# Moving small steps of two attention layers from VectorE to ScalarE, with both halves of a sum in one PSUM tile

## The chip, the cores and the metric

The kernel runs on one core of one Trainium2 chip. The core has five engines, each with its own queue that is worked off in order: PE (TensorE, the matmuls; PEld is its loading of weights), DVE (VectorE), ACT (ScalarE), POOL (GpSimd, here mostly the issue of gathers) and SP (SyncE, the queue of plain transfers). The metric is the device time of one execution in microseconds. One execution was also recorded by the hardware profiler; all durations below are from that record. Lines such as L1364 are lines of the kernel before.

## The reference

The reference is a stack of four graph layers on 3327 nodes with 512 features and one dense 0/1 adjacency matrix with rather few ones. Every layer ends in a residual and a layer norm:

```python
x = _layernorm(x + _L0_gnn_ref(x, adj, W, a1, a2))      # attention, 8 heads of 64
x = _layernorm(x + _L1_gnn_ref(x, adj, ...))            # mean of the neighbours
x = _layernorm(x + _L2_gnn_ref(x, adj, ..., 64))        # mean of the first 64
x = _layernorm(x + _L3_gnn_ref(x, adj, W, a))           # attention, 4 heads of 128

# an attention layer
e = leaky_relu(f1[:, :, None] + f2[:, None, :], 0.2)    # by head, node, neighbour
attention = softmax(where(adj > 0, e, NEG_INF))
out = elu(einsum('hnm,hmo->hno', attention, Wh))

def _layernorm(x):
    return (x - mean(x)) / sqrt(var(x) + 1e-5)
```

Layers 0 and 3 are attention layers, and the change touches these two only.

## The kernel before, in words

The nodes are cut into 26 blocks of 128. For each block the kernel first makes a list of the columns in which the block's rows have a one. A block's list is cut into chunks of 128 places, and up to four chunks make a group (`GROUP`). For each layer there is a table in DRAM with one row per node. An attention layer's row holds, for every head, the projected features and two scores.

**One group** (`Gat.group`, a generator that gives way after each stage) runs as follows. POOL issues one indirect gather per chunk (L1018) into a slot of a ring in SBUF. ACT and DVE make, from list positions, a 0/1 matrix that tells which row of the block each place belongs to (`far` L1316 on ACT, `ds` L1324 and L1326 on DVE). PE multiplies it with the block's own scores (`pg`, L1336 in layer 0 and L1340 in layer 3). DVE adds the neighbours' scores and takes the larger of two (L1353, L1355). ACT takes the exponential twice: once as `w` in PSUM (L1356) and once into the score's column of the gathered rows (L1357), from which the softmax's denominator comes. ACT also makes `sel`, the 0/1 matrix as floats (L1359 or L1361). DVE then multiplies every gathered unit, that is one head's features of one chunk, with its weight (L1364; a group of g chunks has g times 8 units in layer 0, g times 4 in layer 3). At last PE multiplies `sel` with the weighted rows (L1383) and adds into two halves of the heads, `acc[0]` and `acc[1]`. In layer 3 each block's last chunk is preceded by products with the first block as a column (L1380), whose factors come from DVE (`upc`, L1420).

**The halves of a sum.** `Gat.sums` takes two PSUM tiles of one bank each under a tag `acc0` or `acc1`; blocks take turns between the tags. In the last blocks of layer 0 the first block is done densely (`open_dense`, `dense`): its sums (`acct`) hold the tag `acc1`, and all other blocks use the other one.

**The end of a block** (`Gat.summed`, `divided`): DVE takes the two denominators, one instruction for each half (`rden`, L1528), and the reciprocal of both (L1529). ACT divides, head by head (L1532, eight in layer 0, four in layer 3), and makes the exponential of the ELU (L1542). DVE puts together ELU and residual in two passes (L1544, L1546); the second one also gives the row's sum. DVE makes minus the mean from it (`nm`, L1547). ACT squares the difference and sums it (L1548). The inverse root is made by POOL in layer 0 (L1553, L1554) and by ACT and DVE in layer 3 (L1558 to L1564). `scaled_by_act` makes the shift, minus the mean times the inverse root, on DVE (L854), and ACT applies scale and shift (L855). In layer 3 that is the output and SP stores it; in layer 0 the new rows are transposed by PE and multiplied with layer 1's weights (L789, L806).

**What sets the order.** Up to the end of layer 0 a scheduler orders every engine's instructions by its own estimates; there the list building for later blocks runs between the attention of earlier ones. From layer 1 on the order is the one in which the program issues them (`manual_schedule`): the generators of `work` (groups) and `ends` (ends of blocks) are stepped in turn, so the order on each queue is fixed by their `yield`s. Layer 3 starts when layer 2 is done and is the last.

Of the kernel before, what the change touches and what calls it, by code (L numbers as in the profile page):

```python
# [8 lines left out]
F32 = mybir.dt.float32  # L9
# [8 lines left out]
AF = mybir.ActivationFunctionType  # L18
ALU = mybir.AluOpType
# [4 lines left out]
P = 128  # L24
# [581 lines left out]
class Sums(list):  # L606

    turn = 0
# [23 lines left out]
def sparse_path(ctx, tc, flag_i, x, adj, l0_w, l0_a1, l0_a2, l1_w_self, l1_b_self, l1_w_nb, l1_b_nb,  # L632
# [13 lines left out]
    nc = tc.nc  # L646
    N, D = x.shape
# [11 lines left out]
    def pool_in(lay, name, bufs=1, **kw):  # L659
        return lay.enter_context(tc.tile_pool(name=name, bufs=bufs, reuse_waits="tile", **kw))  # L660
# [7 lines left out]
    for b in range(NB):  # L668
        lists.append([])
        if b:  # L670
            n = SEGMENTS[b]
# [179 lines left out]
        nc.vector.tensor_scalar(o, y, mv[:, 0:1], rs, ALU.subtract, ALU.mult)  # L851

    def scaled_by_act(o, y, nm, rs):
        nc.vector.tensor_mul(nm[:, 0:1], nm[:, 0:1], rs)  # L854
        nc.scalar.activation(o, y, AF.Identity, bias=nm[:, 0:1], scale=rs)  # L855


# [181 lines left out]
    class Gat:  # L1039
# [250 lines left out]
        def group(self, item, pools, accs, done, sall=None):  # L1290

            b, l, c0, g, at = item
            ring, sp, pacc, pone = pools
            H, OUT, M = self.H, self.OUT, self.M
            hh = H // 2
# [4 lines left out]
            m = l.places(c0 + g - 1, whole)  # L1300
# [12 lines left out]
            for t, k, q0, q1 in parts:  # L1313
                if q0 < q1:
                    o = t[:, q0 * P:q1 * P] if t is far else t[:, :(q1 - q0) * P]
# [5 lines left out]
            for t, k, q0, q1 in parts:  # L1321
                o, dk = ds[:, q0 * P:q1 * P], dgs[:, l.at, k:k + 1]
# [7 lines left out]
            n = 1 if self.k else 3  # L1330
            pe = pg[:, :GROUP * n * 2 * H].rearrange("p (c k h) -> p c h k", c=GROUP, k=n)
            w = pg[:, GROUP * n * 2 * H:GROUP * (2 * n + 1) * H].rearrange("p (c h) -> p c h", c=GROUP)
# [27 lines left out]
            else:  # L1360
                nc.scalar.activation(S[:, :g], have, AF.Identity)  # L1361
            yield
            Gc = G.rearrange("p c (h m) -> p (c h) m", m=M)
            nc.vector.tensor_mul(Gc[:, :, :OUT], Gc[:, :, :OUT],  # L1364
                                 w[:, :g].rearrange("p c (h o) -> p (c h) o", o=1).to_broadcast([P, g * H, OUT]))
            yield
            while self.held[self.turn] if at == 0 else b not in accs:
                yield
# [3 lines left out]
            for c in range(g):  # L1372
                m = l.places(c0 + c, whole)
# [50 lines left out]
        def sums(self, pacc, turn):  # L1424

            hh = self.H // 2
            self.held[turn] = 1
            acc = Sums(pacc.tile([P, 512], F32, name="acc", tag=f"acc{turn}")[:, :hh * self.M]
                       .rearrange("p (h m) -> p h m", h=hh) for s in range(2))
            acc.turn = turn  # L1430
            return acc

        def open_dense(self, pool, ps, pacc, *spaces):

            H, OUT, M = self.H, self.OUT, self.M
            hh = H // 2
            self.pinned, self.turn = True, 0
            self.up, *self.wt = [t.rearrange("p (h i) -> p h i", i=P) for t in spaces[:3]]  # L1440
            self.gd = spaces[3:]
            f1 = pool.tile([P, H], F32, name="f1c")
            nc.vector.tensor_add(f1, self.fall[:, :H, 0], self.cmax)
            for h in range(H):
                nc.vector.tensor_scalar(self.wt[0][:, h, :], ident, f1[:, h:h + 1], None, ALU.mult)
            yield
            for s in range(2):
                pf = ps.tile([P, hh * P], F32, name="pf", tag="po")
                nc.tensor.matmul(pf, ones, self.wt[0][:, s * hh:(s + 1) * hh], start=True, stop=True)
                nc.scalar.activation(self.up[:, s * hh:(s + 1) * hh], pf.rearrange("p (h i) -> p h i", i=P),  # L1450
                                     AF.Exp, scale=1.0 - GAT_ALPHA)
                yield
            while self.held[1]:
                yield
            self.nil = pool.tile([1, OUT + 1], F32, name="nil")
            nc.vector.memset(self.nil, 0.0)
            self.acc = [pacc.tile([P, hh * P], F32, name="acct", tag="acc1") for s in range(2)]
            for s in range(2):
                nc.tensor.matmul(self.acc[s][:OUT + 1], self.nil, self.up[0:1, s * hh:(s + 1) * hh],
                                 start=True, stop=False)  # L1460
            self.opened = True
# [59 lines left out]
        def divided(self, fin, acc, h):  # L1521

            H, OUT = self.H, self.OUT
            hh = H // 2
            h = h.rearrange("p (s h o) -> p s h o", s=2, h=hh)
            rden = fin.tile([P, 2, hh, 1], F32, name="rden")
            for s in range(2):
                nc.vector.tensor_scalar(rden[:, s], acc[s][:, :, OUT:OUT + 1], 1e-30, None, ALU.max)  # L1528
            nc.vector.reciprocal(rden, rden)  # L1529
            for s in range(2):  # L1530
                for k in range(hh):
                    nc.scalar.activation(h[:, s, k], acc[s][:, k, :OUT], AF.Identity, scale=rden[:, s, k])  # L1532

        def summed(self, fin, acc, xb, space=None):

            hq = acc
            if isinstance(acc, list):
                hq = fin.tile([P, D], F32, name="h") if space is None else space[:, :D]
                self.divided(fin, acc, hq)
                self.held[acc.turn] = 0  # L1540
            e = fin.tile([P, D], F32, name="e") if space is None else space[:, D:]
            nc.scalar.activation(e, hq, AF.Exp)  # L1542
            yield
            nc.vector.scalar_tensor_tensor(hq, hq, 0.0, xb, ALU.max, ALU.add)  # L1544
            nm = fin.tile([P, 2], F32, name="nm")
            nc.vector.scalar_tensor_tensor(e, e, 1.0, hq, ALU.min, ALU.add, accum_out=nm[:, 0:1])  # L1546
            nc.vector.tensor_scalar(nm[:, 0:1], nm[:, 0:1], -1.0 / D, None, ALU.mult)  # L1547
            nc.scalar.activation(hq, e, AF.Square, bias=nm[:, 0:1], accum_out=nm[:, 1:2])  # L1548
            if self.k == 0:
                for _ in range(AHEAD):  # L1550
                    yield
                rs = fin.tile([P, 1], F32, name="rs")
                nc.gpsimd.tensor_scalar(rs, nm[:, 1:2], 1.0 / D, EPS, ALU.mult, ALU.add)  # L1553
                nc.gpsimd.tensor_tensor(rs, rs, mhalf, ALU.pow)  # L1554
                yield
            else:
                r0 = fin.tile([P, 1], F32, name="r0")
                nc.scalar.activation(r0, nm[:, 1:2], AF.Ln, bias=eps, scale=1.0 / D)  # L1558
                nc.scalar.activation(r0, r0, AF.Exp, scale=-0.5)
                yield  # L1560
                rs = fin.tile([P, 1], F32, name="rs")
                nc.vector.scalar_tensor_tensor(rs, nm[:, 1:2], EPS * D, r0, ALU.add, ALU.mult)
                nc.vector.scalar_tensor_tensor(rs, rs, -0.5 / D, r0, ALU.mult, ALU.mult)
                nc.vector.scalar_tensor_tensor(rs, rs, 1.5, r0, ALU.add, ALU.mult)  # L1564
            return e, nm, rs
# [167 lines left out]
    def layer0_end(b, acc):  # L1733
        yield
        x1 = xres[b]
        space = None
        if b == order[-1]:
            while g0.pinned:
                yield
            space = dp.tile([P, H0 * P], F32, name="up")  # L1740
        e, nm, rs = yield from g0.summed(fin, acc, x1, space)
        scaled_by_act(x1, e, nm, rs)
        xt = None
        if space is not None:
            xt = dp.tile([P, H0 * g0.M], F32, name="gd2")[:, :D].rearrange("p (c i) -> p c i", i=P)
        xt = transposed(fin, ps, x1, xt=xt)
        yield
        t2 = fin.tile([P, 2, D], F32R, name="t2", bufs=2)
        po = times(ps, xt, wn)
        nc.scalar.copy(t2[:, 0], po)  # L1750
        nc.vector.tensor_sub(t2[:, 1], po, t2[:, 0].bitcast(F32))
        store(t1_d, b, t2.bitcast(F32).rearrange("p s d -> p (s d)"), 2)
        if b >= NB - LATE0 or not b:
            return
        yield
        zb = fin.tile([P, D], F32, name="zb0", tag="e")
        nc.scalar.copy(zb, times(ps, xt, wx))
        store(z1_d, b, zb)
# [150 lines left out]
    pacc = pool_in(mlay, "l1pa", 2, space=PSUM)  # L1909
# [237 lines left out]
    with ExitStack() as lay:  # L2147
# [7 lines left out]
        def layer3_end(b, acc):  # L2155
            yield
            e, nm, rs = yield from g3.summed(fin, acc, xres[b])
            o = fin.tile([P, D], F32, name="o")
            scaled_by_act(o, e, nm, rs)
            store(out, b, o)  # L2160
# [82 lines left out]
```

## Time and profile before

| what | us |
|---|---|
| median of 4 runs (lowest, highest) | 1757.98 (1748.88, 1762.15) |
| the profiled execution's own time | 1759.4 |
| its span in the profile | 1757.6 |
| busy in the span: PE | 1514.4 (86%) |
| DVE | 1181.8 (67%) |
| ACT | 866.8 (49%) |
| POOL | 752.2 (43%) |
| L1364 in layer 0, 33 groups of 1536 elements (270 to 740 us) | 57.7, mean 1.748 |
| L1364 in layer 3, 24 groups of 1536 elements in one ring part (1480 to 1757 us) | 41.9, mean 1.745 |
| L1547 in layer 0, 26 times | 3.8, mean 0.146 |
| L854 in layer 0, 26 times | 4.0, mean 0.153 |
| L1528 in layer 0, 52 times | 7.6, mean 0.155 |

The span is the time from the first to the last instruction; the profiled execution's own time has 1.8 us more around it. An engine's busy time is a sum over the whole span, in which the four layers have different limits: layer 0's attention lies between about 270 and 740 us, layers 1 and 2 between 740 and 1480, layer 3 behind. So the share of a stretch says more than the share of the span. The profile's chain of waits names the work that ended last at each moment; over the span it is 64% PE, 11% DVE and 7% ACT.

### The profile page before, as it was taken

To read this page: it belongs to the slowest core of one execution; us is meant where nothing else is said; L and a number is where in the kernel's file an instruction comes from. 1 tells how busy PE (TensorE), PEld (TensorE's weight loads), DVE (VectorE), ACT (ScalarE), POOL (GpSimd) and SP (SyncE) were. 2 spreads that over 40 slices of the span, in tenths; PEclk is the share of its full clock that TensorE was granted. 3 is DMA by queue.
4 is the path that set the end of the run, shared out by engine and by line. 5 is a ranking of instruction groups with operands and counts; after the bars stand their busy time and mean duration, and the time that the engine had idled before them with its cause. 6 is when DMAs were issued, how large, how long until landed. Compare 5 with 4: busy or idle time off the path is not lost.

```text
span 1757.6 us, 24418 instructions
## 1 busy us (share of the span) xinstructions
PE 1514.4 (86%) x7307; PEld 1012.4 (58%) x7341; DVE 1181.8 (67%) x3210; ACT 866.8 (49%) x2907; POOL 752.2 (43%) x992
## 2 busy tenths in 40 slices
PE   5789937889999999889999999967999984878885
PEld 4667625656666677545555555423676652756664
DVE  7997857878566789225656776565455553867897
ACT  5788744666666778412212212212444442545686
POOL 2000055555554421163545553276555506666650
PEclk9889968889999999889999999998999995988998
DMA  8877667666664542297888997388767706667771
GB/s 258 266 237 242 211 212 235 212 193 191 207 183 148 170 145 74 94 399 272 291 286 303 339 367 244 99 294 259 244 209 241 256 25 200 183 203 211 215 214 61
DMA packets 120794, 382.01 MB, mean 217 GB/s; under 512 B 22028, under 2 KB 23668, under 8 KB 120650
## 3 DMA queue, kind: packets, MB, share of 16 engines
q0 software_dynamic: 67696, 252.97, 45.7%
q1 hardware_dynamic: 52954, 127.35, 21.6%
q8 instruction: 61, 1.00, 0.2%
q14 instruction: 83, 0.68, 0.1%
HBM read 331.89 MB, written 48.37 MB: 216 GB/s over the span
## 4 chain that ended last, share of the span: by engine, by line
PE 64%; DVE 11%; ACT 7%; issue 7%; DMA 5%; another core or an unknown queue 3%; POOL 3%; SPq 0%; POOLq 0%; ACTq 0%; DVEq 0%
PE po L806 19%; PE acc L1383 13%; PE po L1056 10%; PE acc L1893 9%; PE pt L789 3%; PE acct L1491 1%; PE acc L1885 1%; PE acc L1271 1%; ACT m L882 1%; DVE gt L1364 1%; DVE gl L1364 1%; DMA gt<-t_d,idx 1%; PE acc L1976 1%; DMA ab<-in_adj_dram 1%
## 5 line engine op out<-in xcount | busy, mean ns | idle before, releaser
L1018 POOL DMA_INDIRECT gt<-t_d,idx x201 | 199.4, 992 | 381.3 <-DVE eq L978 209.0
L1018 POOL DMA_INDIRECT gl<-t_d,idx x265 | 263.3, 993 | 201.0 <-issue 57.4
L1383 PE MATMUL acc<-gt,sel 128*128 128x264 f32 (+3 forms) x804 | 213.6, 413 | 4.2 <-issue 2.1
L1018 POOL DMA_INDIRECT gm<-t_d,idx x140 | 140.6, 1004 | 139.7 <-PE acc L1893 89.8
L806 PE MATMUL po<-wn,xt 128*128 128x512 f32 x408 | 194.0, 618 | 7.3 <-ACT xt L792 5.0
L1383 PEld LDWEIGHTS acc<-gt,sel 128*128 128x128 f32 (+3 forms) x804 | 155.3, 202 | 46.0 <-issue 18.2
L1383 PE MATMUL acc<-gl,sel 128*128 128x260 f32 (+3 forms) x524 | 139.1, 409 | 27.6 <-issue 16.8
L1056 PE MATMUL po<-gt,xt 128*128 128x268 f32 x416 | 119.4, 433 | 12.7 <-ACT g0fall L1068 8.2
L806 PEld LDWEIGHTS po<-wn,xt 128*128 128x128 f32 x408 | 77.6, 198 | 91.5 <-issue 82.0
L1364 DVE TENSOR_TENSOR gt<-gt,pg 128x1536 f32<-128x1536 f32 (+3 forms) x64 | 116.6, 1822 | 17.3 <-ACT sel L1359 14.6
L1383 PEld LDWEIGHTS acc<-gl,sel 128*128 128x128 f32 (+3 forms) x524 | 99.4, 200 | 46.6 <-issue 20.1
L796 ACT ACTIVATE xt<-pt 128x128 f32<-128x128 f32 (+1 forms) x208 | 55.8, 291 | 116.9 <-PE pt L789 77.4
L1056 PE MATMUL po<-w,xt 128*128 128x262 f32 x416 | 100.5, 393 | 13.8 <-issue 7.6
L1893 PE MATMUL acc<-gm,selr 128*128 128x512 f32 (+3 forms) x324 | 107.2, 454 | 5.2 <-DMA gm<-t_d,idx 3.8
L792 ACT COPY xt<-pt 128x512 f32<-128x512 f32 x80 | 46.8, 589 | 126.7 <-PE pt L789 103.0
L909 DVE MAX8 cand<-val 128x8 f32<-128x464 uint16 (+32 forms) x184 | 107.5, 619 | 0.1
L1018 POOL DMA_INDIRECT gk<-t_d,idx x65 | 65.6, 1009 | 89.1 <-PE acc L1271 51.6
L789 PE MATMUL pt<-s_ident,xres 128*128 128x128 f32 x500 | 79.1, 286 | 27.0 <-DMA xres<-in_x_dram 12.2
L1316 ACT ACTIVATE far<-place,sites 128x128 int16<-128x128 int16 (+3 forms) x167 | 87.0, 542 | 27.7 <-DVE ds L1326 24.4
L1056 PEld LDWEIGHTS po<-gt,xt 128*128 128x128 f32 x416 | 80.3, 206 | 31.7 <-ACT g0fall L1068 8.6
L806 PE MATMUL po<-wx,xt 128*128 128x512 f32 x208 | 94.3, 597 | 1.7 <-ACT tb L1938 1.2
L1056 PEld LDWEIGHTS po<-w,xt 128*128 128x128 f32 x416 | 78.2, 193 | 29.9 <-issue 9.9
(406 smaller groups left out, 3260.8 us busy)
## 6 DMA issues: line engine op xcount, KB each, us to landing
ab<-in_adj_dram SPq DMA_DIRECT2D x25, 832.0 KB
ab<-in_adj_dram SPq DMA_DIRECT2D x25, 831.5 KB
t_d<-t SPq DMA_DIRECT2D x25, 512.0 KB
gm<-t_d POOLq DMA_DIRECT2D x21, 512.0 KB
t_d<-t SPq DMA_DIRECT2D x25, 384.0 KB
t_d<-tg SPq DMA_DIRECT2D x25, 264.0 KB
gd<-t_d SPq DMA_DIRECT2D x25, 264.0 KB
t_d<-tg SPq DMA_DIRECT2D x25, 260.0 KB
```

Source lines behind the costliest of these rows:

```text
L789: nc.tensor.transpose(pt[:, c, :], src[:, c * P:(c + 1) * P], ident)
L792: nc.scalar.copy(xt, pt)
L796: nc.scalar.activation(xt[:, c, :n], pt[:, c, :n], AF.Identity, accum_out=xsum[:, c, b:b + 1])
L806: nc.tensor.matmul(po, xt[:, c, :], w[:, c], start=c == 0, stop=c == DC - 1)
L882: nc.scalar.activation(m[:, c0:], ab[s][:, c0:], AF.Sign, accum_out=half[:, s, b:b + 1])
L909: nc.vector.max(out=cand[:, s, :], in_=val[:, cuts[s]:cuts[s + 1]])
L1018: nc.gpsimd.indirect_dma_start(out=t[:m, c, :], out_offset=None, in_=table[:, :], in_offset=bass.IndirectOffsetOnAxis(ap=l.idx[:m, c0 + c: ...
L1056: nc.tensor.matmul(pw[s], xt[:, c, :], self.w[:, c, s, :], start=c == 0, stop=c == DC - 1)
L1316: nc.scalar.activation(o, place[:, (c0 + q0) * P:(c0 + q1) * P], AF.Abs, bias=l.nmid[k], scale=2.0)
L1364: nc.vector.tensor_mul(Gc[:, :, :OUT], Gc[:, :, :OUT], w[:, :g].rearrange("p c (h o) -> p (c h) o", o=1).to_broadcast([P, g * H, OUT]))
L1383: nc.tensor.matmul(accs[b][s], S[:m, c, :], G[:m, c, s * hh * M:(s + 1) * hh * M], start=at + c == 0, stop=last)
L1893: nc.tensor.matmul(accs[b], chosen, parts[:, k * D:(k + 1) * D], start=at + c + k == 0, stop=k == top and at + c == n - 1)
```

## The change

The change has four parts.

1. Minus the mean (L1547) and the shift (L854) are made by ACT, with an activation that scales, and no longer by DVE. Both layers use these lines.
2. The two halves of a block's sums are one PSUM tile of two banks, with one buffer for each tag; the dense sums of layer 0 likewise. A tile is guarded as a whole: it comes free when all that read it are done.
3. With both halves in one tile DVE takes both denominators in one instruction.
4. In layer 3 (`self.k` is 1 there and 0 in layer 0) DVE weights all units of a group but the last; ACT weights that one, with the weight that it has put into the score's column itself.

```diff
     def scaled_by_act(o, y, nm, rs):
-        nc.vector.tensor_mul(nm[:, 0:1], nm[:, 0:1], rs)
+        nc.scalar.activation(nm[:, 0:1], nm[:, 0:1], AF.Identity, scale=rs)
         nc.scalar.activation(o, y, AF.Identity, bias=nm[:, 0:1], scale=rs)
...
             Gc = G.rearrange("p c (h m) -> p (c h) m", m=M)
-            nc.vector.tensor_mul(Gc[:, :, :OUT], Gc[:, :, :OUT],
-                                 w[:, :g].rearrange("p c (h o) -> p (c h) o", o=1).to_broadcast([P, g * H, OUT]))
+            n = g * H - self.k
+            nc.vector.tensor_mul(Gc[:, :n, :OUT], Gc[:, :n, :OUT],
+                                 w[:, :g].rearrange("p c (h o) -> p (c h) o", o=1)[:, :n].to_broadcast([P, n, OUT]))
+            if n < g * H:
+                nc.scalar.activation(Gc[:, n, :OUT], Gc[:, n, :OUT], AF.Identity, scale=Gc[:, n, OUT:OUT + 1])
...
-            acc = Sums(pacc.tile([P, 512], F32, name="acc", tag=f"acc{turn}")[:, :hh * self.M]
-                       .rearrange("p (h m) -> p h m", h=hh) for s in range(2))
+            both = pacc.tile([P, 2, 512], F32, name="acc", tag=f"acc{turn}", bufs=1)
+            acc = Sums(both[:, s, :hh * self.M].rearrange("p (h m) -> p h m", h=hh) for s in range(2))
             acc.turn = turn
+            acc.both = both[:, :, :hh * self.M].rearrange("p s (h m) -> p s h m", h=hh)
...
-            self.acc = [pacc.tile([P, hh * P], F32, name="acct", tag="acc1") for s in range(2)]
+            acct = pacc.tile([P, 2, 512], F32, name="acct", tag="acc1", bufs=1)
+            self.acc = [acct[:, s, :hh * P] for s in range(2)]
...
-            for s in range(2):
-                nc.vector.tensor_scalar(rden[:, s], acc[s][:, :, OUT:OUT + 1], 1e-30, None, ALU.max)
+            if isinstance(acc, Sums):
+                nc.vector.tensor_scalar(rden, acc.both[:, :, :, OUT:OUT + 1], 1e-30, None, ALU.max)
+            else:
+                for s in range(2):
+                    nc.vector.tensor_scalar(rden[:, s], acc[s][:, :, OUT:OUT + 1], 1e-30, None, ALU.max)
...
-            nc.vector.tensor_scalar(nm[:, 0:1], nm[:, 0:1], -1.0 / D, None, ALU.mult)
+            nc.scalar.activation(nm[:, 0:1], nm[:, 0:1], AF.Identity, scale=-1.0 / D)
```

## The prediction

> **What bounds the kernel now.** I read the busy time by stretches first, to find where DVE, the engine that the change relieves, could be the one that ends last. Columns: length, then busy us of PE, PEld, DVE, ACT, POOL, then granted clock, DMA share, GB/s.
>
> ```profile
> 270.00:400.00 130.00, 107.14 (x565) 76.33 (x563) 105.80 (x317) 77.92 (x229) 71.73 (x76) 0.88 0.68 209
> 400.00:640.00 240.00, 230.38 (x1113) 159.36 (x1112) 166.15 (x419) 165.38 (x545) 116.78 (x135) 0.98 0.59 178
> 640.00:740.00 100.00, 93.96 (x495) 66.30 (x495) 69.80 (x145) 70.95 (x264) 10.30 (x15) 0.95 0.24 77
> ```
>
> ```profile
> 1545.00:1660.00 115.00, 96.63 (x600) 78.42 (x600) 89.12 (x258) 69.86 (x212) 72.80 (x75) 0.90 0.73 207
> 1660.00:1740.00 80.00, 64.12 (x440) 53.22 (x439) 74.06 (x233) 61.93 (x194) 29.96 (x31) 1.00 0.56 165
> ```
>
> The first three are layer 0's attention, the last two layer 3's. From 400 to 640 PE is busy 230.4 of 240 us: nothing taken from DVE there shortens the span by more than PE's idle 9.6 us. PE's idle time is 22.9 us in 270-400 and 6.0 us in 640-740. Only in 1660-1740 is DVE the busiest (74.1 of 80), with ACT close behind (61.9). So I read that stretch instruction by instruction. Columns: start, duration, engine, line, operation, tiles, shapes.
>
> ```profile
> 1676.80 0.17 DVE L1355 TENSOR_TENSOR sc<-sc 128x12 f32<-128x12 f32 x1
> ...
> 1677.11 0.22 DVE L1528 TENSOR_SCALAR rden<-acc 128x2 f32<-128x2 f32 x2
> ...
> 1677.81 0.16 DVE L1564 SCALAR_TENSOR_TENSOR rs<-rs,r 128x1 f32<-128x1 f32 x1
> 1678.01 0.16 DVE L854 TENSOR_TENSOR nm<-nm,rs 128x1 f32<-128x1 f32 x1
> 1678.08 1.75 DVE L1364 TENSOR_TENSOR gl<-gl,pg 128x1536 f32<-128x1536 f32 x1
> ...
> 1680.25 0.69 DVE L1544 SCALAR_TENSOR_TENSOR h<-h,xres 128x512 f32<-128x512 f32 x1
> ...
> 1681.59 0.08 DVE L1546 DVE_READ_ACCUMULATOR e<-e,h 128x1 f32 x1
> 1681.71 0.15 DVE L1547 TENSOR_SCALAR nm<-nm 128x1 f32<-128x1 f32 x1
> 1681.78 1.13 DVE L1420 SCALAR_TENSOR_TENSOR upc<-upc,least,col 128x128 f32<-128x128 f32 x4
> ```
>
> ```profile
> 1677.06 0.18 ACT L1356 ACTIVATE pg<-sc 128x12 f32<-128x12 f32 x1 [1.17 <-remote]
> ...
> 1679.59 0.63 ACT L1542 ACTIVATE e<-h 128x512 f32<-128x512 f32 x1
> 1680.12 0.80 ACT L855 ACTIVATE o<-e,nm,rs 128x512 f32<-128x512 f32 x1
> ...
> 1683.07 0.20 ACT L1559 ACTIVATE r<-r 128x1 f32<-128x1 f32 x1
> 1684.44 0.18 ACT L1356 ACTIVATE pg<-sc 128x12 f32<-128x12 f32 x1 [1.17 <-DVE sc L1353]
> ```
>
> The reader is to see a loop, once per block: ACT's exponential (L1356, 1677.06) runs on to e (L1542, ends 1680.22), which DVE's L1544 follows at 1680.25: **leg A, 3.19 us**. DVE then runs L1544, L1546, L1547, L1420, L1364 and the scores, and ACT's next exponential starts at 1684.44: **leg B, 4.19 us**. Together 7.38 us a block (7.58 in the next, which has one more 0.2 us zero copy on ACT). In leg B ACT idles 1.17 us before that exponential.
>
> **The change, part by part.** Line numbers are those of the kernel before. PE, POOL and SP keep their instructions. In the built program DVE loses 155: 52 of L854, 52 of L1547 (26 blocks in each of two layers) and 51 of L1528. ACT gains 104 in place of the first two, and 57 weightings.
>
> *Layer 3, DVE.* L1364 loses 128 of its elements. The groups of 1536 and 2048 elements took 1.747 and 2.277 us, so 512 elements cost 0.530 and 128 cost 0.13 us. L1547 leaves: L1420 started 0.07 us after it, and it 0.12 after the accumulator read; without it I put 0.10 saved. L854 leaves: it started 0.20 after L1564 on which it depended, and L1364 does not, so about 0.13 to 0.20 goes. Two L1528 of 2 columns become one of 4 (about 0.1 less). Per block with two groups: 0.26 + 0.10 + 0.2 + 0.1 = 0.66 us of DVE.
>
> *Layer 3, ACT.* It gains two 128x1 operations and two 128x128 weightings a block. For the first the nearest rows are L1559 (0.20 us) and the 128x8 ones of L1479 (0.207); followed by what depends on them I put 0.22 each. For the second it is the same operation on another tile:
>
> ```profile
> L1408 ACT ACTIVATE gcol<-gcol x4: 386/386/388, 1467.9 to 1468.7; 128x128 f32<-128x128 f32 x4
> ```
>
> Four of them in a row started 0.27 us apart, so 0.27 is what a queue of independent work pays and 0.39 the other end. I take 0.27, since the weighting stands between independent operations. Sum 2 x 0.22 + 2 x 0.27 = 0.98 us; by the upper ends 2 x 0.21 + 2 x 0.39 = 1.2.
>
> *Both together in the loop.* All four new ACT operations fall into leg B: the built order has L854 before L855, a weighting before each L1356, and L1547 before the square. Leg A keeps its ACT work, 3.19. Leg B on DVE is 4.19 - 0.10 - 0.13 = 3.96 (only one of the two L1364 is in it). Leg B on ACT, start to start in the trace: L855 0.71, two exponentials 0.19, sel 0.31, far 0.57, square and its read 0.84, Ln 0.33, Exp 0.11: 3.06; with the new work 4.04, begun 0.13 before leg B, so over at 3.91. The two engines end almost together and the loop takes 7.15 to 7.2 in place of 7.38. **I take 0.2 us a block**, on the nine full periods of the tail: -1.8 us. Most of DVE's 0.66 is not on the path: what goes in leg A is covered by ACT's 3.19.
>
> The Trainium skill ("ScalarE: Activation LUTs", Rules for kernel authors) speaks against the move: multiplications belong on VectorE, and an ACTIVATE should be budgeted at some 0.3 us and 0.83 ns an element. Estimated by that page the four would cost 2 x 0.3 + 2 x 0.41 = 1.42 us, leg B on ACT would be 4.35 and the loop 7.54, a loss of 0.16 a block. The rows above are shorter, so the sum stays with them.
>
> *From 1545 to 1660* the loop is a different one: PE waits for L1364, and DVE's scores wait for PE (PE restarts at 1640.39 and 1649.52, with 4.9 of the 9.1 us on DVE). 0.10 + 0.13 = 0.23 us a block is on it. Ten blocks end here; PE is at full load in some and at half clock in others, so I count half: -1.2 (ends 0 and -2.3). Between 1497 and 1545 gathers and PE decide: 0. At the very end each last block's chain keeps two more hops inside ACT: 2 x 0.05, +0.1.
>
> *PE's new wait.* The last matmul of a group now waits for ACT's weighting too; behind it stands PE's whole queue. The weighting before the first L1356 comes 1.2 us after PE starts that group's 2.9 us, and only the product of the last chunk's second half needs it. Cost nothing; with that cover gone, up to 0.3 us a block.
>
> *Layer 0.* DVE loses 26 x (0.15 + 0.15 + 0.15) = 11.7 us, ACT gains 26 x 0.4 = 10. DVE also loses a stall:
>
> ```profile
> DVE nm L854 <- POOL rs L1554: 17.0, 15, 2.0
> ```
>
> (us in all, times, longest.) ACT inherits this wait; L855, right behind L854, had it already through DVE (10.7 us in 10 waits). In 400-640 PE covers all of it. Four blocks end in 270-400, where PE waited 10.3 us for L1364: 4 x 0.3 = -1.2. Six end in 640-740 with ACT as full as DVE (70.9 and 69.8): I put -0.8. The single guard of both halves makes a block's first matmul wait for eight L1532 instead of four, some 4 x 0.24 = 1 us, but two turns alternate and PE has dense products between; nothing, or +1 for each of six blocks. Layer 0's order is made by the scheduler, and it moves: at two places, the list building around 300-400 and the dense part's end, matmuls swap by a few tens. I cannot price that from rows beyond the idle time: -6 to +4, taken as 0. Layer 0: **-2**.
>
> **Sum:** -1.8 - 1.2 + 0.1 - 2.0 = -4.9 us, from the profiled execution's 1759.4 us (span 1757.6) to **1754.5**; from the median of the four runs, 1758.0, it would be 1753.
>
> **Rivals.** *DVE alone decides.* If ACT's new work hides wholly and leg A follows DVE, the tail gains 0.66 on nine blocks (-5.9), 1545-1660 -2.3, layer 0 -2 to -8 by PE's waits for DVE: about -13, 1746. For it: DVE 93% busy in the tail. Against: e ended 0.03 us before L1544 started, so ACT holds leg A. *ACT takes over (slower).* If each new operation costs its full duration and 0.1 us of hand-over, 1.2 + 0.4 = 1.6 us in place of 0.98, leg B on ACT ends at 4.53; it decides from 4.19, that is from 1.26 us of added work. That is 0.34 on 21 blocks, +7, and in layer 0's dense end 6 x 0.4 = +2.4: 1769. For it: 61.9 us of ACT already in 80. Against: the 0.27 us spacing. *Nothing moves:* PE, gathers and clock set the end and what is gained is waited for: 1759.
>
> **How the numbers follow.** Forecast 0.48, DVE alone 0.22, ACT takes over 0.16, nothing 0.14. A measurement of this kernel can tell about 0.5% (8.8 us) from no change. The forecast's own spread (-9 to 0) gives 0.04 to faster; so faster 0.26, within 0.5% 0.58, slower 0.16. The range 1744 to 1767 takes in the first rival and most of the second.
>
> **What would show it.** Right: in the tail L1544 follows L1544 by 7.15 to 7.45 us, ACT's wait before L1356 falls from 1.17 to under 0.2, and L1364 of 12 units takes 1.61. Wrong: ACT's wait stays near 1 us (gain larger), or DVE waits for ACT at the scores (loss); layer 0's end (last L1554 at 721.6 us) moved by over 4 us shows that the scheduler's order mattered.

## The result and the profile after

The changed kernel takes **1759.39 us** (median of 52 runs, 1751.62 to 1768.79) against 1755.76 us of the kernel before (78 runs, 1744.17 to 1770.58): ratio **1.0019, 95% interval 1.0008 to 1.0031**. It is slower by some 3 us. The forecast was 5 us of gain: the range held, the sign did not. Two later measurements of both kernels gave 1.0023 (1.0006 to 1.0041) and 1.0007 (0.9979 to 1.0034).

The profiled execution after has a span of 1760.5 us (1757.6 before). In the kernel after, lines from L1364 on lie a little lower: the weighting by DVE is L1365 and that by ACT L1368, the products L1386, the denominators of both halves L1533 (at least 1e-30 each), the division L1540, e L1550, the two ELU passes L1552 and L1554, minus the mean L1555, POOL's root L1561 and L1562, the dense products L1496, their closing L1513 and the dense transposes L1521.

Busy time by stretches of the kernel after (columns as in the prediction: length, PE, PEld, DVE, ACT, POOL, clock, DMA share, GB/s):

```profile
270.00:400.00 130.00, 103.83 (x579) 75.02 (x579) 107.19 (x316) 80.92 (x241) 73.35 (x77) 0.95 0.69 209
400.00:640.00 240.00, 229.50 (x1112) 158.28 (x1110) 163.22 (x367) 173.58 (x586) 124.03 (x136) 0.99 0.59 177
640.00:740.00 100.00, 88.69 (x457) 63.45 (x456) 62.30 (x117) 68.18 (x256) 7.53 (x13) 0.90 0.21 67
1545.00:1660.00 115.00, 94.14 (x585) 75.61 (x584) 81.55 (x217) 78.54 (x247) 73.35 (x76) 0.89 0.73 211
1660.00:1740.00 80.00, 68.45 (x451) 55.13 (x450) 68.88 (x206) 72.12 (x239) 32.92 (x34) 0.96 0.62 176
```

In layer 3's tail (last line) the load moved as the change says: DVE 74.1 to 68.9, ACT 61.9 to 72.1, and PE is busy 4.3 us longer in the same 80 us, with 451 matmuls for 440; a part of the 4.3 us is the lower clock (0.96 for 1.00). In layer 0's end (640 to 740) it is the other way round: PE does 457 matmuls for 495 and is busy 5.3 us less, although its clock is lower (0.90 for 0.95), and no other engine is fuller than before.

Periods of the tail's loop after, first DVE, then ACT (start, duration, engine, line, operation, tiles; in brackets idle time and releaser):

```profile
1680.73 0.16 DVE L1572 SCALAR_TENSOR_TENSOR rs<-rs,r 128x1 f32<-128x1 f32 x1
1680.81 1.61 DVE L1365 TENSOR_TENSOR gl<-gl,pg 128x1408 f32<-128x1408 f32 x1
...
1683.22 0.69 DVE L1552 SCALAR_TENSOR_TENSOR h<-h,xres 128x512 f32<-128x512 f32 x1 [0.32 <-issue]
...
1690.59 0.69 DVE L1552 SCALAR_TENSOR_TENSOR h<-h,xres 128x512 f32<-128x512 f32 x1 [0.54 <-issue]
...
1705.58 0.69 DVE L1552 SCALAR_TENSOR_TENSOR h<-h,xres 128x512 f32<-128x512 f32 x1 [0.42 <-issue]
...
1714.65 0.69 DVE L1552 SCALAR_TENSOR_TENSOR h<-h,xres 128x512 f32<-128x512 f32 x1 [0.53 <-ACT e L1550]
```

```profile
1680.04 0.18 ACT L1356 ACTIVATE pg<-sc 128x12 f32<-128x12 f32 x1 [0.51 <-DVE sc L1355]
...
1683.10 0.28 ACT L854 ACTIVATE nm<-nm,rs 128x1 f32<-128x1 f32 x1
1683.41 0.81 ACT L855 ACTIVATE o<-e,nm,rs 128x512 f32<-128x512 f32 x1
1684.13 0.39 ACT L1368 ACTIVATE gl<-gl 128x128 f32<-128x128 f32 x1
1684.42 0.16 ACT L1356 ACTIVATE pg<-sc 128x8 f32<-128x8 f32 x1
...
1687.23 0.16 ACT L1356 ACTIVATE pg<-sc 128x12 f32<-128x12 f32 x1
...
1711.05 0.18 ACT L1356 ACTIVATE pg<-sc 128x12 f32<-128x12 f32 x1 [1.37 <-PE pg L1340]
```

L1552 follows L1552 by 7.37 us (before 7.58 at the same place, with two zero copies on ACT), ACT's wait ahead of L1356 has gone from 1.17 to 0.51 and then to nothing, and now it is DVE that idles ahead of L1552. The last two DVE lines and the last ACT line show a period that went otherwise: it takes 9.07 us, and in it ACT waits 1.37 us for PE. With it the tail as a whole, from the first ELU pass of the eleventh block from the end to the end of the span, takes 77.3 us for 77.4 before.

In layer 0 the last two roots on POOL started at 721.62 and 725.62 us before and at 726.61 and 731.05 after (the 721.6 in the prediction, called the last, is the last but one). At layer 0's last gather the kernel after was still ahead: it started at 639.6 us, that of before at 645.1. So these two traces, one of each kernel, put what was lost into layer 0's end; layer 3 won a part of it back: from its first product with weighted rows (at 1473.0 us, before at 1466.5) to the end of the span it took 287.5 us for 291.2.

### The profile page after: what moved, and what is told of

Its sections match the earlier page's. It is cut to its first block, busy times and chain, and to the rows that moved or that the text cites. A ratio compares the mean times of both kernels' runs of the same rounds, so it can differ in the third digit from the quotient of the medians.

```text
span 1760.5 us, 24428 instructions
## 1 busy us (share of the span) xinstructions
PE 1509.9 (86%) x7307; PEld 1010.1 (57%) x7341; DVE 1160.1 (66%) x3055; ACT 904.2 (51%) x3068; POOL 759.8 (43%) x992
## 4 chain that ended last, share of the span: by engine, by line
PE 62%; ACT 11%; DVE 9%; issue 9%; DMA 4%; POOL 2%; another core or an unknown queue 2%; SPq 0%; ACTq 0%; DVEq 0%; POOLq 0%
PE po L806 20%; PE acc L1386 12%; PE po L1056 10%; PE acc L1901 9%; PE pt L789 3%; PE acc L1893 1%; DVE gt L1365 1%; ACT h L1540 1%; PE acc L1271 1%; DVE cand L909 1%; DMA gd<-t_d 1%; ACT far L1316 1%; PE acct L1496 1%; ACT h L1556 1%
## 5 line engine op out<-in xcount | busy, mean ns | idle before, releaser
L1018 POOL DMA_INDIRECT gt<-t_d,idx x201 | 204.2, 1016 | 360.5 <-DVE eq L978 208.0
L1386 PE MATMUL acc<-gt,sel 128*128 128x264 f32 (+3 forms) x804 | 206.8, 404 | 4.7 <-DVE gt L1365 3.0
L1386 PEld LDWEIGHTS acc<-gt,sel 128*128 128x128 f32 (+3 forms) x804 | 151.7, 197 | 47.5 <-issue 20.8
L1386 PE MATMUL acc<-gl,sel 128*128 128x260 f32 (+3 forms) x524 | 141.4, 414 | 16.1 <-issue 7.7
L1365 DVE TENSOR_TENSOR gt<-gt,pg 128x1536 f32<-128x1536 f32 (+3 forms) x64 | 116.7, 1824 | 17.5 <-ACT sel L1359 15.2
L1386 PEld LDWEIGHTS acc<-gl,sel 128*128 128x128 f32 (+3 forms) x524 | 101.1, 203 | 35.6 <-issue 11.0
L789 PEld LDWEIGHTS pt<-s_ident,xres 128*128 128x128 f32 x500 | 61.9, 146 | 59.5 <-issue 27.6
```

The costliest lines, as they stand in the source:

```text
L789: nc.tensor.transpose(pt[:, c, :], src[:, c * P:(c + 1) * P], ident)
L1018: nc.gpsimd.indirect_dma_start(out=t[:m, c, :], out_offset=None, in_=table[:, :], in_offset=bass.IndirectOffsetOnAxis(ap=l.idx[:m, c0 + c: ...
L1365: nc.vector.tensor_mul(Gc[:, :n, :OUT], Gc[:, :n, :OUT], w[:, :g].rearrange("p c (h o) -> p (c h) o", o=1)[:, :n].to_broadcast([P, n, OUT]))
L1386: nc.tensor.matmul(accs[b][s], S[:m, c, :], G[:m, c, s * hh * M:(s + 1) * hh * M], start=at + c == 0, stop=last)
```

## The experiments

Theory 1, after seeing this: layer 3's part gains what the two chains say or a little more, and layer 0's part loses more. For layer 0 there were two theories. **Work:** the operations given to ACT, and the one tile that comes free only as a whole, cost the time. **Order:** the scheduler, given other instructions or tiles, puts layer 0's instructions in another order, and that order is worse. In the traces some 250 of the 3443 matmuls ahead of layer 1's first gather are in another place (counted by line and tile names). All ratios are against the kernel before, run on the same chip beside it; the chips differ, and are called A to D.

**One layer at a time** (chip A; before 1644.05 us). Each part of the change was made in one layer only, by the layer's number `self.k`, as here for minus the mean; e3 has `if not self.k` in all places:

```diff
-            nc.scalar.activation(nm[:, 0:1], nm[:, 0:1], AF.Identity, scale=-1.0 / D)
+            if self.k:
+                nc.scalar.activation(nm[:, 0:1], nm[:, 0:1], AF.Identity, scale=-1.0 / D)
+            else:
+                nc.vector.tensor_scalar(nm[:, 0:1], nm[:, 0:1], -1.0 / D, None, ALU.mult)
```

e2, layer 3 only; layer 0's matmuls are in the order of before:

> All four parts of the change in layer 3 alone; layer 0 has the lines of the kernel before, and its built order is the same instruction by instruction on PE. Theory 1 (layer 3 gains what the tail's loop shows, 7.37 us a block in place of 7.58, and layer 0's new order loses more): 4 to 6 us faster than before, ratio 0.997, and layer 3 from its first sel to the end 4 to 5 us shorter. Rival 2 (layer 3 gains nothing in the mean, the whole change is lost there): within 1 us of before. Rival 3 (layer 3 itself is what got slower): 3 us slower, ratio 1.002.

Measured: 1639.36 us, ratio 0.9973 (0.9956 to 0.9989).

e3, layer 0 only; layer 0's order is that of the changed kernel:

> The change in layer 0 alone (minus the mean, shift, one tile, one rden); layer 3 as before. PE's built order is that of the changed kernel. Theory 1: 7 to 9 us slower than before, ratio 1.0045, all of it between the last gather of layer 0 (640 us) and the last inverse root (726 us in the profile before, 731 after). Rival 2: 3 to 4 us slower. Rival 3: the time of before within 1 us.

Measured: 1658.04 us, 1.0089 (1.0064 to 1.0114), more than expected. So the gain and the loss are both there, and the loss is all in layer 0.

**Layer 0 taken apart** (chip A). e4 has in layer 0 only minus the mean and the shift on ACT; e5 only the one tile, with one instruction for both denominators.

> In layer 0 only ACT makes minus the mean and the shift; two tiles and two rden as before; layer 3 as before. The scheduler gives a third order. If ACT's 0.4 us of new work a block is what costs in layer 0: 5 to 8 us slower, like the whole layer 0 part. If the guard of the one tile costs: the time of before or 1 to 2 us faster, since DVE is freed. If only the order counts: any time between -5 and +8, with a PE stall in the dense part in its own place.

Measured: 1651.4 us, 1.0040 (1.0024 to 1.0056).

> In layer 0 only the one tile for both halves with one rden; ACT and DVE keep minus the mean and the shift; layer 3 as before. If the guard costs (a block's first matmul waits for all eight divisions): 4 to 8 us slower. If ACT's new work costs: the time of before or 1 to 3 us faster. If only the order counts: any time between -5 and +8, not the sum's complement to the other part.

Measured: 1652.7 us, 1.0051 (1.0031 to 1.0071). Either half loses, though they have no instruction in common. What they share is that the order changes: by line and tile names in the traces 142 and 111 matmuls stand elsewhere, in e2 and e6 one.

**Smaller pieces and a piece without work** (chip B; before 1746.0 us).

> The whole change again, beside the kernel before on one chip. If the part in layer 0 and the part in layer 3 add up as the two kernels with one layer changed were measured (1.0089 and 0.9973), the ratio is 1.006, some 10 us more. If layer 3's gain hides in part behind what layer 0 loses, or the loss depends on the chip, it is nearer to the first measurement's 1.002 (3 us).

Measured: 1749.24 us, 1.0023 (1.0006 to 1.0041): nearer to the first measurement than to the 1.006 of the sum.

e7 and e8: of layer 0's two moves to ACT only one each, minus the mean (L1547) or the shift (L854).

> Layer 0 alone, and there only minus the mean on ACT: some fifteen short activations, and 68 matmuls of layer 0 in another place, nearly all in the dense end. Theory work (the operations moved to ACT cost the time): about 0.2 us of 0.5 us a block of what both moves cost together, so +2.5 to +3 us of 6.6. Theory order (the scheduler's new order of the matmuls costs the time, above all in the dense end): most of the loss is already here, +4 to +7 us, if the dense end is what matters; 0 to +2 us if the other reordered place (300 to 400 us) is.

Measured: 1748.85 us, 1.0026 (1.0000 to 1.0053).

> Layer 0 alone, and there only the shift on ACT: as many short activations of 0.28 us, and 179 matmuls in another place, nearly the places in which the kernel with both moves has them. Theory work: +3.5 to +4 us, and this one and the one with minus the mean add up to 6.6. Theory order: the same loss as both moves together, +5 to +7 us, and the two do not add up.

Measured: 1751.29 us, 1.0039 (1.0016 to 1.0061). e8 alone has the loss of e4, and the two would add up to 1.0065, against e4's 1.0040. That leans to order, but the intervals are too wide to decide.

e9: in layer 0 the sums in one tile as in the change, but the two instructions for the denominators as before (the expectation calls them guard instructions; the tile itself still comes free only as a whole):

```diff
+            both = pacc.tile([P, 2, 512], F32, name="acc", tag=f"acc{turn}", bufs=1)
...
             for s in range(2):
                 nc.vector.tensor_scalar(rden[:, s], acc[s][:, :, OUT:OUT + 1], 1e-30, None, ALU.max)
```

> Layer 0 alone, and there only the one tile for both halves' sums, with the two guard instructions of before: no instruction is added, dropped or moved to another engine, but 168 matmuls are in another place, nearly all in the dense end. Theory work: 0 to +1 us (nothing is done that was not done before). Theory order: +2 to +8 us with no work changed.

Measured: 1754.8 us, **1.0063** (1.0037 to 1.0089). No instruction more or less, none on another engine, and yet a loss of some 11 us by the ratio (8.8 by the medians), and on another chip (e9b below) 1.0030. Work in the sense of busy time cannot be the reason here; the order can, or the coarser waits of one tile.

**Order without tiles or operations** (chip C; before 1646.35 us). e14 and e15 move only a `yield` in `dense`, the generator of layer 0's dense rows, so the instructions and the tiles are those of before:

```diff
# e14: one yield more
+            yield
             nc.vector.tensor_tensor(wt[:m], self.up[:m], fs[:m, 1, :, None].to_broadcast([m, H, P]), ALU.max)
# e15: one yield less, ahead of the dense matmuls
             nc.vector.tensor_mul(wt[:m], wt[:m], row0[:m, j, None, :].to_broadcast([m, H, P]))
-            yield
```

> The kernel before with one more yield in the dense rows of layer 0, between ScalarE's weighting of the rows and VectorE's making of their weights: the same instructions, 409 matmuls in another place, all in 500 to 720 us. Theory work: 0, within 1 us. Theory order: a change of the same size as the other reordered kernels, +3 to +12 us; if the order of before is not a good one but any one, it may as well be a gain of some us.

Measured: 1654.75 us, **1.0055** (1.0034 to 1.0075).

> The kernel before with one yield less in the dense rows of layer 0, between VectorE's making of the weights and the matmuls: the same instructions, 351 matmuls in another place, all in 500 to 720 us. Theory work: 0, within 1 us. Theory order: +3 to +12 us, or a gain of some us if the order of before is not a good one.

Measured: 1644.73 us, 0.9988 (0.9972 to 1.0005): as fast as before, with 351 matmuls in another place. So the same instructions in another order can cost 9 us, which is theory order's claim; but being reordered is not enough, there are harmless orders too.

e13: two idle activations more per block in layer 0:

```diff
+            if not self.k:
+                nc.scalar.activation(fin.tile([P, 1], F32, name="spare"), eps, AF.Identity, scale=1.0)
             nc.scalar.activation(e, hq, AF.Exp)
```

> The kernel before with two idle activations more in each block of layer 0 (128x1, into tiles that nobody reads: one just ahead of the exponential of the block's sums, one behind its square). All that layer 0 did it still does, in the same order: 2 matmuls in another place. ScalarE has as many short operations more as the changed kernel gave it there. Theory work: about the loss of the kernel that has the two ACT operations in layer 0, +4 to +7 us. Theory order: 0 to +1 us.

Measured: 1645.22 us, 0.9996 (0.9982 to 1.0010). By its expectation that would be against theory work. The profile takes this back. The lines' own view of e13 (duration ns, then first and last start):

```profile
L1551 ACT ACTIVATE spare<-s_eps x26: 185/187/195, 241.5 to 255.1; 128x1 f32<-128x1 f32 x26
```

All 26 ran between 241.5 and 255.1 us, and so did the other 26, long before the ends of blocks that they were written into: they wait for nothing, so the scheduler put them first. The run shows that 10 us of ACT at that place cost nothing that can be told. It says nothing on ACT work in the ends of the blocks, and **theory work is not refuted for the moves to ACT (e4, e7, e8)**.

e6: layer 3's part alone, without ACT's weighting of the last unit (L1364 as before):

> Layer 3 alone, without ScalarE's weighting of each group's last unit: one tile with one guard, minus the mean and the shift on ACT. Layer 0 is as before. By the two chains of layer 3's loop the DVE leg falls from 4.19 to about 4.09 us without the weighting, so that the DVE leg still decides and the loop is about 7.3 us for 7.38: -1 us in all. If it has the whole gain of layer 3 (-4.5 us), the weighting was worth nothing and the three small operations off DVE were the gain; if it has none, the weighting was the gain.

Measured: 1638.65 us, **0.9963** (0.9947 to 0.9979). The whole gain of layer 3 is there without the weighting. The loop of the tail in e13, whose layer 3 is that of before, then in e6 (start of the first ELU pass):

```profile
1562.75 0.69 DVE L1554 SCALAR_TENSOR_TENSOR h<-h,xres 128x512 f32<-128x512 f32 x1 [0.35 <-ACT e L1552]
...
1608.33 0.68 DVE L1554 SCALAR_TENSOR_TENSOR h<-h,xres 128x512 f32<-128x512 f32 x1
```

```profile
1551.57 0.69 DVE L1559 SCALAR_TENSOR_TENSOR h<-h,xres 128x512 f32<-128x512 f32 x1 [0.58 <-ACT e L1557]
...
1595.86 0.68 DVE L1559 SCALAR_TENSOR_TENSOR h<-h,xres 128x512 f32<-128x512 f32 x1
```

Six periods take 45.58 us in e13, 44.29 in e6, and 44.08 in e2 (1554.34 to 1598.42): the three small steps off DVE (with the one tile) are worth 1.3 us here, the weighting 0.2. The loop repeats closely enough for such a reading: in six traces of chips A and C with layer 3 as before, the tail takes 77.7 to 77.9 us. Ahead of the tail the weighting brings a wait of its own. What PE waited for from 1405 to 1660 us, first in e2 (with the weighting, L1371 there), then in e6 (us in all, times, longest):

```profile
PE acc L1389 <- ACT gl L1371: 6.5, 7, 2.4
PE acc L1389 <- ACT r L1576: 5.3, 5, 1.2
```

```profile
PE acc L1389 <- ACT r L1577: 8.8, 8, 1.4
PE acc L1389 <- issue: 7.1, 7, 2.2
```

PE's wait for ACT's weighted unit (with the 2.3 us for ring part gk, 8.8 us) takes the place of the others (in e13 they are 13.3 us for `r` and 10.5 of issue): from layer 3's first product to the end PE idles 23.8 us in all in e2 and 25.4 in e6, for 27.8 to 32.3 in the six kernels with the layer 3 of before.

**Where in layer 0?** (Chip D, before 1757.31 us; later on the same chip, before 1757.43 us.) The traces pointed to the last piece. PE's matmuls of it, before and after:

```profile
713.25 0.69 PE L1516 MATMUL acc<-s_ident,raw 65*128 65x65 f32 x4
...
715.03 3.25 PE L1383 MATMUL acc<-gt,sel 128*128 128x264 f32 x8
718.11 3.60 PE L806 MATMUL po<-wn,xt 128*128 128x512 f32 x8
723.26 0.66 PE L789 MATMUL pt<-s_ident,xres 128*128 128x128 f32 x4 [1.55 <-ACT xres L855]
```

```profile
715.00 1.97 PE L1386 MATMUL acc<-gt,sel 128*128 128x264 f32 x4
716.76 1.07 PE L1521 MATMUL acc<-s_ident,raw 65*128 65x65 f32 x8
...
719.50 5.35 PE L806 MATMUL po<-wn,xt 128*128 128x512 f32 x8
728.39 0.66 PE L789 MATMUL pt<-s_ident,xres 128*128 128x128 f32 x4 [3.55 <-ACT xres L855]
```

Before, the dense block's transposes of the first half come right behind the closing, ahead of the last ordinary block's products, and its end runs beside these. After, they come in the midst of them: with the dense sums in one tile ACT's copy of the first half started at 714.20, as the closing of both halves ended (714.17), where before it started at 711.65, ahead of the second half's (713.32). ACT's copies before, then after:

```profile
711.65 0.58 ACT L1512 COPY raw<-acct 65x512 f32<-65x512 f32 x1 [2.59 <-PE acct L1508]
713.36 0.58 ACT L1512 COPY raw<-acct 65x512 f32<-65x512 f32 x1 [1.12 <-PE acct L1508]
```

```profile
714.20 1.07 ACT L1517 COPY raw<-acct 65x512 f32<-65x512 f32 x2 [5.60 <-PE acct L1513]
```

Both blocks' ends then fall together and PE stands 3.55 us for 1.55. From the end of the closing to layer 1's first gather it is 30.5 us for 26.1; in e3 28.5, in e14 29.4, in e13 26.3. **Theory tail** said that this is the loss. Three kernels test it: e16 makes only this swap in the kernel before, e17 undoes only it in the changed kernel, e19 has one tile in turn 0 only, so that the dense rows are ordered as in e9 and the tail as before.

```diff
# e16, the kernel before
+            yield
             acc = self.sums(pacc, 1)
             for h in range(H):
                 nc.tensor.transpose(acc[h // hh][:, h % hh, :OUT + 1],
# e17, the changed kernel
-            acct = pacc.tile([P, 2, 512], F32, name="acct", tag="acc1", bufs=1)
-            self.acc = [acct[:, s, :hh * P] for s in range(2)]
+            self.acc = [pacc.tile([P, hh * P], F32, name="acct", tag="acc1") for s in range(2)]
```

> The kernel before with one yield more ahead of the dense block's eight transposes: the same instructions and tiles, and 24 matmuls in another place, all behind the closing of the dense sums (the transposes come behind the last ordinary block's matmuls, as in the changed kernel). Theory tail: from the closing to layer 1's first gather 28 to 30 us for 26.1, the longest wait of PE for the normalized block 3 to 4 us for 1.6, and +2 to +4.5 us in all. Theory elsewhere (the loss comes from the order ahead of the closing): 0, within 1 us.

Measured: 1757.89 us, 1.0003 (0.9980 to 1.0026). The swap did what it should to the tail, as PE's lines of e16 show:

```profile
709.02 3.73 PE L1386 MATMUL acc<-gt,sel 128*128 128x264 f32 x8
712.54 1.07 PE L1522 MATMUL acc<-s_ident,raw 65*128 65x65 f32 x8
...
722.21 0.66 PE L789 MATMUL pt<-s_ident,xres 128*128 128x128 f32 x4 [3.34 <-ACT xres L855]
```

The transposes are late, PE waits 3.34 us, and from the closing to the first gather it takes 30.6 us; the median moves by 0.6 us.

> The changed kernel, but the dense sums that are transposed, and the sums of the turn that shares their space, lie in two tiles again in layer 0: 10 matmuls behind the closing go back to the order of before, the order ahead of it stays nearly that of the changed kernel. Theory tail: -2 to -4.5 us against the changed kernel of the same call, and about as fast as before or faster, since layer 3 gains 4.5 to 6. Theory elsewhere: the same as the changed kernel, within 1 us.

Measured: 1762.16 us, 1.0031 (1.0007 to 1.0055). The order of the tail is back, its length in part (2.48 us of wait for 3.55, 27.8 us to the first gather for 30.5), and the time is not: the changed kernel on the same chip, next, is 4.8 us faster.

> The changed kernel once more, for comparison in one call: 1.001 to 1.004 of the kernel before, as in the two calls before.

Measured: 1757.35 us, 1.0007 (0.9979 to 1.0034).

> The kernel before with one tile for both halves' sums in turn 0 of layer 0 only; turn 1 and the dense sums keep two tiles. The same instructions and the transposes in their old place; 152 matmuls in another place, nearly all of the dense rows, some 30 to 80 us ahead of the closing. If this order costs by itself: as much as the kernel with both turns in one tile, +6 to +11 us. If it costs only with late transposes, or if the tail is the cause: 0, within 2 us.

Measured (chip D, later, with e9 beside it): 1760.27 us, 1.0017 (0.9989 to 1.0045).

> The kernel with one tile in both turns of layer 0 and two guards once more, on the chip of the kernel with one tile in turn 0 only: 1.004 to 1.009, as before.

Measured: 1763.76 us, 1.0030 (1.0003 to 1.0057). So theory tail is not borne out: alone the swap is worth 0.5 us, though with an interval from -3.5 to +4.6 that still holds the +2 to +4.5 expected, and undoing it gained nothing where -2 to -4.5 was expected. And those 4.5 us would be too few for e3's 14.6. The order of the dense rows alone (e19) is not told from nothing either, nor from e9b.

e18 (chip D): e6 with one yield less, as in e15.

> Layer 3's part without ScalarE's weighting (measured 0.9963) and one yield less in layer 0's dense rows (measured 0.9988, not told from 1). If they add up 0.995; if the yield is worth nothing 0.996 to 0.997.

Measured: 1751.93 us, 0.9963 (0.9938 to 0.9987): as e6. Layer 3's part and the yield were not measured alone on this chip, so which of them gains here is open. The best ratio to the kernel before is that of **e6**, the change in layer 3 alone, without the weighting; it was not measured beside the changed kernel.

## Why the prediction was wrong, by its steps

- **The loop of layer 3's tail: right.** L1365 of 11 units takes 1.61 us as said, and in the periods shown the loop takes 0.21 us less. Leg B takes 4.01 us (1683.22 to 1687.23) for the 3.96 put down for DVE and 3.91 for ACT; ACT has no idle time in it, so it is ACT that ends last. Put at -1.8 us; e2's six periods gained 1.50, so nine about -2.2. But this is the gain on chips A and C. In the one trace of the changed kernel the 9.07 us period eats it. A period of over 8.7 us stands in all five traces of a changed layer 3 on the other chips, in three of seven there with the layer 3 of before, and in none of A and C. The granted clock from 1660 to 1700 us was 0.91 in the changed kernel and 1.00 before; that it is the cause was not tried.
- **1545 to 1660: right in kind, too small.** All of layer 3 was put at -2.9; e2 gives -4.4 (0.0027 of 1644) and e6 -6.1 (0.0037 of 1646), each give or take 2.7. In their traces the tail takes 75.8 and 76.2 us for 77.7 to 77.9 in the six kernels of A and C with the layer 3 of before, and what lies ahead of it in layer 3 takes 163.7 and 164.6 for 166.5 to 168.7. So about 2 us were gained in the tail and 2 to 5 ahead of it, where 1.2 was put, with 2.3 as the upper bound.
- **Which of the steps pays: wrong.** The weighting was counted with 0.13 us a block on the path. It is worth 0.2 us in six blocks of the tail, and over the layer no gain by it can be told (e6 against e2, on two chips).
- **PE's new wait "cost nothing": not settled.** The wait came: 8.8 us in e2 for ACT's weighted units. But it took the place of other waits, so whether it eats the weighting's gain is not shown.
- **ACT's price: nearly right, and the rival "ACT takes over" did not come.** From start to start L1555 takes 0.22, L854 0.31 and L1368 0.29: 0.22 + 0.31 + 2 x 0.29 = 1.11 us a block for the 0.98 put down, and below the 1.26 from which that rival began. A part of the 0.13 is a misreading: the four rows of L1408 start at 1467.86 to 1468.73, which is 0.29 apart and not 0.27. The estimate by the Trainium skill, ScalarE: Activation LUTs (Rules for kernel authors), was 1.42 and a slower loop. Its price for one activation is near what L854 and L1368 take by themselves here (0.28 and 0.39 us, by the rule 0.30 and 0.41); but the next activation starts 0.29 us after a weighting, ahead of the weighting's end. The measured rows decide against the estimate.
- **Layer 0 at -2: this is the step that failed,** and in it the sentence that the scheduler's order could not be priced, "-6 to +4, taken as 0". Measured alone layer 0's part is +14.6 us on chip A (e3). In the changed kernel it is some +8, from +3.3 in all less layer 3's -4.4, if layer 3 gains there what it gained on chip A; the two traces give -3.7 for it and so some +7. All are outside the bounds that were given. The prediction's own sign of it, layer 0's end moved by over 4 us, is there (5.0 and 5.4 us), in one trace of each kernel.
- **"The single guard: nothing, or +1 a block": right as to that wait, but the one tile did something else.** In the changed kernel's layer 0 no product waits for a division; only its weight loads do, 0.4 us in 2 waits (1.0 in 3 before). Yet the tile by itself loses (e5, and e9 with the denominators as before): it makes ACT's copy above wait for both halves, and the scheduler orders the dense rows anew. Which of these costs, and how, is not shown.
- **ACT "inherits" DVE's stall on POOL's root: right, but it grew:**

```profile
ACT nm L854 <- POOL rs L1562: 26.0, 20, 3.7
```

It was 17.0 us in 15 waits on DVE (us in all, times, longest). Behind it now stand ACT's steps for the dense rows, for which PE waits in turn (1.4 us at once, `PE acct L1496 <- ACT nm L854`).

What stays open is *why* layer 0 loses, and *where* only in part. The traces of chips A and C narrow it down. From layer 0's first gather to layer 1's first one the four kernels without a loss in layer 0 (e2, e6, e13, e15) take 474.1 to 481.2 us, the four with one (e3, e4, e5, e14) 482.4 to 485.6; from layer 0's last gather on it is 91.5 to 96.6 and 97.6 to 101.4. PE idles 32.4 to 35.7 and 36.5 to 45.2 us in layer 0. By the means the difference is 6.5 us in layer 0, 4.5 of them behind the last gather, and a part of it is PE waiting. In layers 1 and 2 the two groups do not differ (697.6 to 701.2 and 698.7 to 702.0 us).

That another order of the same instructions can lose as much is shown (e14, without any change of tiles). Why e14's does and e15's does not is not. Whether the moves to ACT lose by their order or by the longer way through ACT was not separated, since e13 missed its place; nor was the order that the one tile brings told from the waits for both halves. And the two layers' parts add up to 1.006 where the whole was measured three times at 1.001 to 1.002. The parts were measured on a chip with a higher clock (below), which may be the reason; this was not tried. Layer 3's gain, too, is clear only on A and C: on the other chips it took 286.0 to 292.5 us in five traces with a changed layer 3 and 285.9 to 294.2 in seven with that of before.

## What to carry to other kernels

Where a scheduler orders the instructions, the cost of a small edit is not the sum of its instructions: compare the built orders first, prefer places where the order is fixed or stays as it was, and time an edit that changes the order alone to learn what a new order costs. A long wait that appears in the trace together with a loss is a suspect and no more: make that wait alone and undo it alone. And look in the profile at where an added idle instruction ran before reading anything from its run.

## What the runs showed of the hardware

- The kernel before took 1644 and 1646 us on chips A and C and 1746 to 1757 on the others; the granted clock in the profiled runs was 0.955 to 0.960 on the former and 0.921 to 0.937 on the latter.
- Runs of one kernel follow that clock too, loosely: e9's spans went from 1747.3 us at 0.937 over 1750.9 at 0.930 to 1759.5 at 0.924, but one took 1762.2 at 0.929. A profile of one execution differs by several us from the next in stretches that the edit does not touch: layer 3 as before took 244.3 to 246.6 us in six traces of A and C, and 285.9 to 294.2 in seven of the others. So places of a loss under 5 us cannot be read from two profiles of the latter.
- On ACT an activation of 128x1 takes 0.19 to 0.21 us with a constant as scale and no bias from a tile (L1555, e13's idle ones), 0.28 us with a scale read from a tile (L854) and 0.29 with a bias read from one (L1558 of the kernel before).
